# Reordering the last products of a convolution layer, and trimming idle products between layers, in a two-layer fp32 kernel

## The chip, the cores and the metric

The kernel runs on one core of a Trainium2 chip. The metric is the device time of one execution in microseconds (us). Three executions of the kernel before were timed; their median stands for it. A separate execution was profiled, and all instruction times below are from that one, counted from the start of its span.

## The reference, cut to what matters

```python
def reference(x, ...):                 # x: 32 images, 1024 channels, 14 x 14
    x = x + layer0(group_norm(x))      # three look-up products with softmax
    x = x + layer1(group_norm(x))      # linear attention and a depthwise 3x3
    return x

def layer0(x):
    out = relu(bn(amm(x, c1, lut1)))               # 1024 -> 256 channels
    out = relu(bn(amm(patches3x3(out), c2, lut2))) # 256 -> 256 channels
    return relu(bn(amm(out, c3, lut3)) + x)        # 256 -> 1024 channels

def amm(patches, centroids, lut):
    # per codebook: scores against 16 centroids, softmax, product with a table
    scores = 2 * einsum("blcs,cks->blck", v, centroids) - sum(centroids ** 2)
    return einsum("blck,cko->blo", softmax(scores), lut)
```

Batch normalisation takes its statistics over all images, so each of the three products of layer 0 must be complete before the next one can start. All is fp32.

The text calls the three products of layer 0 "layer 1", "layer 2" and "layer 3" of the kernel, as the code does, and the attention layer "layer 4".

## The kernel before, in words

**Units.** Layers 1 and 2 run over 16 pairs of images (392 positions) and, in each pair, over 8 blocks of 512 score rows: 128 units each, numbered u. For a unit, TensorE computes four score tiles of 128 x 392 (L874 in layer 1; L994 and L1003 in layer 2), called S(u) below. ScalarE takes their exponentials (L566). VectorE turns them so that the 16 scores of a codebook lie side by side (L578), sums them (L596), takes the reciprocal (L598) and turns that back (L604). GpSimd multiplies (L608); in layer 1 it also adds the two halves of the scores (L581) ahead of VectorE's sum. In units whose number divides by four GpSimd first writes a block of rows to a spare tile (L606). SyncE copies rows of the spare tile into every 16th row of the unit's tiles by DMA (L694), four copies or three. Then TensorE multiplies the unit with the table (L712), called L(u) below: eight matmuls, or six in every fourth unit, accumulated over the eight units of a pair. A matmul of fp32 shows as two instructions.

**Order.** Each engine executes its instructions in the order in which the program writes them, and `units` writes this order by hand: a loop over i in which S(i+4), the first transpose of unit i+3, the softmax of unit i+2 and L(i) follow each other in layer 1 (S(i+3), transpose and softmax of i+2, and L(i) in layer 2). `side(i)` hangs further work on the loop: group normalisation, and from i = 121 loads of layer 2's tables, 512 KB each, into the buffers that layer 1's tables leave.

**Between layers 1 and 2.** After L(127) come batch statistics, scale and bias (L749, L310 to L327). `store_pair(p, h)` writes the normalised map of a pair into a padded tile on ScalarE (L904) and sends it to DRAM in three DMAs (L915). `load_patches` reads the shifted maps back (L935), on SyncE's queue and, for the first unit, on ScalarE's too. In the list `luts2[b]`, entry 1 loads a table, entry 2 subtracts its last rows from the others with two matmuls and two copies on ScalarE (L669, L670), entry 3 keeps a piece of it in DRAM (L673) and entry 4 loads pieces from there (L676). Score biases need one more matmul (L388) and several small operations on VectorE, which also makes the score matrices w8 (L349) and wm (L975).

**Between layers 2 and 3.** `relu3(k, b)` normalises one chunk of 448 positions on ScalarE (L1078), `score3` computes four score tiles (L1088) and their exponentials. The products of layer 3 are at L1123.

**Layer 4** begins with residual, normalisation statistics and group normalisation of the first pair. Its instructions are put in order by a planner (`Plan`), which gives each piece a rank and an assumed duration and lets each engine take the ready piece of the lowest rank.

**Products nobody reads.** `warm(n, rhs)` writes n matmuls of the identity with some tile (L561; L1344 in layer 4). Their results aren't used.

Of the kernel before, what the change touches and what calls it, by code (L numbers as in the profile page):

```python
# [21 lines left out]
N2 = 2 * HW  # L22
# [128 lines left out]
def conv_preact_kernel(ctx: ExitStack, tc: tile.TileContext, a: dict, out: bass.AP):  # L151
# [3 lines left out]
    NP = B // 2  # L155
# [335 lines left out]
    def layers(exact, early=None):  # L491
# [20 lines left out]
        pads = [  # L512
            big.tile([P, 2 * IMG], F32, tag=f"pad{k}", name=f"pad{k}") for k in range(2)
        ]
# [42 lines left out]
        def warm(n, rhs):  # L557

            t = scores(rhs.shape[1])
            for _ in range(n):  # L560
                nc.tensor.matmul(t, ident, rhs, start=True, stop=True)  # L561
# [131 lines left out]
            for j in range(0 if q else 1, 4):  # L693
                nc.sync.dma_start(t[15::16, j, :N2], kept[4 * q + j - 1 :: 16])  # L694

        def units(ahead, ts, pool, luts, score, bias, dst, stats, side, last, halve=False):

            n = 8 * NP  # L700
            po, late, tts = [], [], {}

            def lut(u):
                p, b = divmod(u, 8)
                if b == 0:
                    po[:] = [
                        ps_po.tile([P, 512], F32, tag="po", name="po")[:, :N2] for h in range(2)
                    ]
                j0 = 0 if b % 4 else 1
                order = [(h, j) for h in range(2) for j in range(j0, 4)]  # L710
                for h, j in order if b == 7 else sorted(order, key=lambda k: k[1]):
                    nc.tensor.matmul(  # L712
                        po[h],
                        luts[b][:, j, h * P : (h + 1) * P],
                        ts[u % len(ts)][:, j, :N2],
                        start=(b == 0 and j == j0),
                        stop=(b == 7 and j == 3),
                    )
                if b == 7:
                    for h in range(2):  # L720
                        o = dst[:, h, p * N2 : (p + 1) * N2]
                        nc.scalar.copy(o, po[h])
                        late.append((stats[:, h, p, :], o))

            for i in range(-ahead, n):
                u = i + ahead
                if u < n:
                    scs = score(u)
                    exponentials(ts[u % len(ts)], scs, bias[:, 4 * (u % 8) :][:, :4])
                u = i + ahead - 1  # L730
                if 0 <= u < n:
                    tts[u] = token_major(pool, ts[u % len(ts)], halve)
                u = u - 1 if halve else u
                if 0 <= u < n:
                    softmax(
                        pool,
                        u,
                        ts[u % len(ts)],
                        *tts.pop(u),
                        spare=spares[u // 4 % 2] if u % 4 == 0 else None,  # L740
                    )
                    spare_rows(ts, u)
                while late:
                    nc.vector.bn_stats(*late.pop(0))
                side(i)
                if i >= 0:
                    lut(i)
            for h in range(2):
                nc.vector.bn_stats(*late.pop(0))  # L749
                last(h)  # L750
# [4 lines left out]
        with ExitStack() as s:  # L755
# [55 lines left out]
            luts2 = [packed_lut(2, b) for b in range(8)]  # L811
# [19 lines left out]
            luts = [packed_lut(1, b) for b in range(8)]  # L831
# [24 lines left out]
            ts = unit_tiles(AHEAD + 2)  # L856
# [11 lines left out]
            def score1(u):  # L868
# [18 lines left out]
                side,  # L887
                lambda h: bn_final(once, stats1, 1, [h], sc1, bi1),
                halve=not exact,
            )  # L890
            add_up(0, 8 * NP)


        with ExitStack() as s:
# [48 lines left out]
            luts2[0][2]()  # L943
            luts2[0][3]()
            luts2[1][2]()
            luts2[7][1]()
            load_patches(0, 0, 1, engines=(nc.sync, nc.scalar))
            store_pair(0, 1)
            luts2[2][2]()
            load_patches(0, 1, 3)  # L950
            luts2[3][2]()
            for b in range(4):
# [14 lines left out]
            )  # L967
            w8 = score_matrices(once, 2, "8", raw8, mask64)
            biases()
            warm(5, pads[0][:, :N2])  # L970

            centre(once, 2, "1", raw1, 2.0)
            wm = once.tile([P, 2, 4, P], F32, tag="wm", name="wm")
# [38 lines left out]
            ahead = 1 if exact else 3  # L1012
# [28 lines left out]
            out2 = out1  # L1041
# [19 lines left out]
        with ExitStack() as s:  # L1061
            once = s.enter_context(tc.tile_pool(name="p3c", bufs=1))
            stats3 = once.tile([P, CT, NCH, 6], F32, tag="stats3", name="stats3")
            mv3 = once.tile([P, CT, 2], F32, tag="mv3", name="mv3")
            again = None
            sf = s.enter_context(tc.tile_pool(name="p3t", bufs=4))
            st = s.enter_context(tc.tile_pool(name="p3tt", bufs=2))
            ap = s.enter_context(tc.tile_pool(name="p3a", bufs=2))
            luts = luts3
            w3, bias3 = parts[3]  # L1070

            def chunk(k, b):
                return out2[:, b, k * NC : (k + 1) * NC]

            def relu3(k, b):
                if k < NCH:
                    v = chunk(k, b)
                    nc.scalar.activation(  # L1078
                        v, v, AF.Relu, bias=bi2[:, b : b + 1], scale=sc2[:, b : b + 1]
                    )  # L1080

            def score3(k, b):
                v = chunk(k, b)
                scs = []
                for j in range(4):
                    sc = scores(NC)
                    r = slice(32 * j, 32 * j + 32)
                    nc.tensor.matmul(  # L1088
                        sc, w3[r, b, :], v[r], start=True, stop=True
                    )  # L1090
                    scs.append(sc)
                t = sf.tile([P, 4, NC], F32, tag="t", name="t")
                exponentials(t, scs, bias3[:, 4 * b : 4 * b + 4])
                return t

            for k, b in ((0, 0), (0, 1), (1, 0), (1, 1)):
                relu3(k, b)
            warm(7, out2[:, 0, :N2])
            t3, nxt = [score3(0, 0), score3(0, 1)], [score3(1, 0)]
            warm(5, out2[:, 0, :N2])  # L1100
            for b, t in enumerate(t3):
                softmax(st, b, t, *token_major(st, t))
            for k in range(NCH):
                more = k + 1 < NCH
                if more and k:
                    nxt = [score3(k + 1, 0)]
                elif not more and not exact:
                    add_up(2, 2 * NCH)
                    again = overflow(once)
                if early and k > 0:  # L1110
                    early.pop(0)(ps_tr)
                o = ap.tile([P, CT, NC], F32, tag="o3", name="o3")

                for ms in ((0, 1, 2), *((m,) for m in range(3, CT))) if k == 0 else (
                    (m,) for m in range(CT)
                ):
                    pos = [
                        ps_po.tile([P, 512], F32, tag="po", name="po3")[:, :NC] for m in ms
                    ]
                    for h in range(2):  # L1120
                        for m, po in zip(ms, pos):
                            for g in range(4 * h, 4 * h + 4):
                                nc.tensor.matmul(  # L1123
                                    po,
                                    luts[g][:, m * P : (m + 1) * P],
                                    t3[h][:, g % 4, :],
                                    start=(g == 0),
                                    stop=(g == 7),
                                )
                    for m, po in zip(ms, pos):  # L1130
                        nc.scalar.copy(o[:, m, :], po)  # L1131
                        nc.vector.bn_stats(stats3[:, m, k, :], o[:, m, :])  # L1132
                        if not more:
                            bn_sum(mv3[:, m, :], stats3, m)
                        if more and m == 0:
                            nxt.append(score3(k + 1, 1))
                        if m in (4, 5):
                            relu3(k + 2, m - 4)
                        if more and m in (1, 3):
                            t = nxt[m // 2]  # L1140
                            softmax(st, 2 * k + 2 + m // 2, t, *token_major(st, t))
                nc.sync.dma_start(o3d[:, :, k * NC : (k + 1) * NC], o)
                t3 = nxt
            bn_final(once, None, 3, range(CT), sc3, bi3, mv3)
# [20 lines left out]
    with ExitStack() as s:  # L1165
# [188 lines left out]
        def group_norm(p, h, rank):  # L1354
# [3 lines left out]
            key = lambda n: (n, p % 2, h)  # L1358
# [44 lines left out]
            do(DVE, rank, 0.1, variance, [pv], [key("gve")])  # L1403
            if p == 0 and h == 1:

                for n, need in ((16, []), (10, [key("gve")])):
                    warm(n, need)
            do(
                POOL, rank, 1.9, scale, [key("gve"), key("nmc")], [key("ga"), key("gb")], port=True
# [338 lines left out]
        def store(p, h, xt, rank):  # L1748
# [23 lines left out]
            key=8.5,  # L1772
# [176 lines left out]
```

## Time and profile before

| what | value |
|---|---|
| median of 3 runs | 3738.24 us (3735.01 to 3738.82) |
| the profiled execution | 3735.15 us, its span 3733.4 us |
| granted TensorE clock, mean | 0.994 |
| TensorE busy (matmuls) | 3640.7 us, 98% |
| VectorE busy | 2981.7 us, 80% |
| GpSimd busy | 2303.4 us, 62% |
| ScalarE busy | 1715.1 us, 46% |
| layer 1's last product ends | 835.6 us |
| layer 2's first and last products | 875.28 us, 1840.7 us |
| layer 3's first product, and its end | 1861.51 us, 2569.7 us |

A line of the timeline reads: start in us, length in us, engine, line of the kernel, operation, output <- input, shape, number of instructions, and in brackets the idle time ahead of it with what ended it. SPq and ACTq are the DMA issues on SyncE's and ScalarE's queues. A granted clock of 1.00 is TensorE's full speed. Where several instructions stand in one line, its length is that of the whole group.

### The profile page before, as it was taken

To read this page: it belongs to the slowest core of one execution; us is meant where nothing else is said; L and a number is where in the kernel's file an instruction comes from. 1 tells how busy PE (TensorE), PEld (TensorE's weight loads), DVE (VectorE), ACT (ScalarE), POOL (GpSimd) and SP (SyncE) were. 2 spreads that over 40 slices of the span, in tenths; PEclk is the share of its full clock that TensorE was granted. 3 is DMA by queue.
4 is the path that set the end of the run, shared out by engine and by line. 5 is a ranking of instruction groups with operands and counts; after the bars stand their busy time and mean duration, and the time that the engine had idled before them with its cause. 6 is when DMAs were issued, how large, how long until landed. Compare 5 with 4: busy or idle time off the path is not lost. (4 is left out here: it accounts for less than half of the span.)

```text
span 3733.4 us, 49281 instructions
## 1 busy us (share of the span) xinstructions
PE 3640.7 (98%) x16231; PEld 2030.0 (54%) x16231; DVE 2981.7 (80%) x4287; ACT 1715.1 (46%) x3883; POOL 2303.4 (62%) x1394
## 2 busy tenths in 40 slices
PE   8999999998999999999999999998999999999998
PEld 4555555554444444445444444445666666666665
DVE  8999999988888888888734333333699999999996
ACT  5555555543333333333312122213766676666774
POOL 6999999983445445445311111111988888878886
PEclk9999999999999999999999999999999999999999
DMA  3111111115343434344211111103133233322321
GB/s 109 43 46 44 43 43 37 32 54 128 82 94 79 94 78 94 79 97 83 62 40 48 40 40 40 40 22 131 33 87 94 77 86 89 86 85 82 89 74 44
DMA packets 235329, 256.51 MB, mean 69 GB/s; under 512 B 32240, under 2 KB 232816, under 8 KB 235064
## 3 DMA queue, kind: packets, MB, share of 16 engines
q1 hardware_dynamic: 234280, 252.88, 25.7%
q8 instruction: 132, 2.16, 0.3%
q14 instruction: 133, 1.09, 0.1%
q10 hardware_dynamic: 784, 0.37, 0.0%
HBM read 164.04 MB, written 77.09 MB: 65 GB/s over the span
## 5 line engine op out<-in xcount | busy, mean ns | idle before, releaser
L608 POOL TENSOR_TENSOR t<-t,r 128x1664 f32<-128x1664 f32 (+2 forms) x284 | 1006.8, 3545 | 975.5 <-DVE r L604 780.5
L712 PE MATMUL po<-t,lut 128*128 128x392 f32 x3840 | 1331.2, 499 | 5.1 <-DMA t<-spare 5.1
L712 PEld LDWEIGHTS po<-t,lut 128*128 128x128 f32 x3840 | 709.8, 190 | 594.9 <-issue 122.5
L566 ACT ACTIVATE t<-sc,cbias 128x392 f32<-128x392 f32 (+1 forms) x1136 | 579.1, 593 | 886.9 <-issue 480.5
L1459 PE MATMUL mm<-y,lut 128*128 128x392 f32 x2048 | 713.9, 495 | 2.8 <-ACT y L1425 1.7
L1123 PE MATMUL po<-t,lut 128*128 128x448 f32 x1792 | 680.6, 540 | 3.7 <-POOL t L608 2.1
L578 DVE STREAM_TRANSPOSE tt<-t 128x1664 f32<-128x1664 f32 (+1 forms) x284 | 541.9, 1908 | 111.8 <-ACT t L566 102.5
L604 DVE STREAM_TRANSPOSE r<-rc 128x1664 f32<-128x1664 f32 (+1 forms) x284 | 546.6, 1925 | 20.9 <-DVE rc L598 0.5
L1681 DVE SCALAR_TENSOR_TENSOR pa<-y,lepe_w,pa 128x406 f32<-128x406 f32 x900 | 538.9, 638 | 5.3 <-PE pa L1663 2.6
L1123 PEld LDWEIGHTS po<-t,lut 128*128 128x128 f32 x1792 | 338.2, 190 | 343.1 <-issue 340.3
L1459 PEld LDWEIGHTS mm<-y,lut 128*128 128x128 f32 x2048 | 370.4, 188 | 250.3 <-issue 8.0
L596 DVE TENSOR_REDUCE sm<-tt 128x104 f32<-128x832 f32 (+2 forms) x284 | 423.4, 1491 | 7.5 <-POOL tt L581 2.0
L1132 DVE BATCH_NORM_STATS2 stats<-o 128x6 f32<-128x448 f32 x112 | 69.0, 617 | 450.0 <-ACT o L1131 450.0
L581 POOL TENSOR_TENSOR tt<-tt 128x832 f32<-128x832 f32 x128 | 247.7, 1935 | 9.3 <-DVE tt L578 9.3
L1131 ACT COPY o<-po 128x448 f32<-128x448 f32 x112 | 59.0, 528 | 405.1 <-PE po L1123 359.1
L598 DVE RECIPROCAL rc<-sm 128x104 f32<-128x104 f32 (+1 forms) x284 | 229.5, 808 | 9.8
L994 PE MATMUL sc<-patch,cw 64*128 64x392 f32 x1024 | 204.9, 514 | 2.3 <-ACT lut L670 1.4
L609 ACT ACTIVATE sm<-sm 128x104 f32<-128x104 f32 (+1 forms) x284 | 84.8, 299 | 221.2 <-DVE rc L598 219.2
L1644 POOL TENSOR_TENSOR qr<-qr,zb 128x784 f32<-128x784 f32 x64 | 117.4, 1850 | 59.6 <-DMA zb<-zd 52.2
L1312 ACT ACTIVATE w<-x,tb,gn_a 128x196 f32<-128x196 f32 x248 | 128.3, 517 | 49.2 <-DVE x L1326 34.7
L994 PEld LDWEIGHTS sc<-patch,cw 64*128 64x128 f32 x1024 | 87.9, 184 | 110.8 <-issue 63.4
L606 POOL TENSOR_TENSOR spare<-t,r 128x392 f32<-128x392 f32 x64 | 65.1, 1017 | 120.1 <-DMA patch<-h1d 31.6
(189 smaller groups left out, 4090.3 us busy)
## 6 DMA issues: line engine op xcount, KB each, us to landing
patch<-h1d SPq DMA_DIRECT2D x248, 162.8 KB
x<-in_x_dram SPq DMA_DIRECT2D x32, 784.0 KB
o3d<-o SPq DMA_DIRECT2D x14, 1792.0 KB
x<-in_x_dram SPq DMA_DIRECT2D x64, 392.0 KB
out_dram<-x SPq DMA_DIRECT2D x64, 392.0 KB
o<-o3d SPq DMA_DIRECT2D x62, 392.0 KB
h1d<-pad SPq DMA_DIRECT2D x96, 225.0 KB
t<-spare SPq DMA_DIRECT2D x960, 12.2 KB
```

Of the source, the lines that this page charges most:

```text
L566: nc.scalar.activation(t[:, j, : sc.shape[1]], sc, AF.Identity if exact else AF.Exp, bias=bias[:, j : j + 1],)
L578: nc.vector.transpose(tt, tf)
L581: nc.gpsimd.tensor_tensor(tv[:, :, :8], tv[:, :, :8], tv[:, :, 8:], ALU.add)
L596: nc.vector.tensor_reduce(sm, tv, AX.X, ALU.add)
L598: nc.vector.reciprocal(rc, sm)
L604: nc.vector.transpose(r, bc(rc, 2, KC))
L608: nc.gpsimd.tensor_tensor(tf, tf, r, ALU.mult)
L712: nc.tensor.matmul(po[h], luts[b][:, j, h * P : (h + 1) * P], ts[u % len(ts)][:, j, :N2], start=(b == 0 and j == j0), stop=(b == 7 and j = ...
L994: nc.tensor.matmul(sc, w8[r, 8 * h + 4 * (j // 2) + g], grid(pbuf[n % NPB][r, j // 2, g]), start=True, stop=False,)
L1123: nc.tensor.matmul(po, luts[g][:, m * P : (m + 1) * P], t3[h][:, g % 4, :], start=(g == 0), stop=(g == 7),)
L1459: nc.tensor.matmul(pv(), w[kt][:, m0 : m0 + P], ywin(p, first + kt), start=(kt == 0), stop=(kt == 3),)
L1681: nc.vector.scalar_tensor_tensor(acc, neighbours(p, c, offset(k)), lw[:, c, k : k + 1], acc, ALU.mult, ALU.add,)
```

## The change

- `units` has a new argument `near`. In layer 1 (of the normal path) it is 8 x 16 - 12 = 116. Up to i = 115 the loop writes L(i) as before; at i = 116 it writes L(116) and L(117); after that it writes L(i+1). The statistics of the last outputs are held back in the last turn, so that they are written after the loop as before. In layer 2 `near` isn't given and the order stays.
- Between layers 1 and 2, `luts2[2][2]()` (two matmuls and two copies on ScalarE) moves ahead of the load of the eighth table, of the first patch loads and of `store_pair(0, 1)`. `warm(5)` ahead of the first scores goes.
- Between layers 2 and 3, `warm(7)`, which read the normalised map, becomes `warm(3)` on a table, ahead of everything; `relu3` of the second chunk goes behind the first chunk's scores and exponentials.
- In layer 4 the two groups of unread products have 12 and 9 instead of 16 and 10.

```diff
@@ units
-                while late:
+                while late and i < n - 1:
                     nc.vector.bn_stats(*late.pop(0))
                 side(i)
-                if i >= 0:
-                    lut(i)
+                near = n if near is None else near
+                for u in (i, i + 1) if i == near else (i + 1,) if i > near else (i,):
+                    if 0 <= u < n:
+                        lut(u)
@@ layer 1's call of units
                 halve=not exact,
+                near=None if exact else 8 * NP - 12,
@@ layer 1 to 2
             luts2[1][2]()
+            luts2[2][2]()
             luts2[7][1]()
             load_patches(0, 0, 1, engines=(nc.sync, nc.scalar))
             store_pair(0, 1)
-            luts2[2][2]()
             load_patches(0, 1, 3)
...
             biases()
-            warm(5, pads[0][:, :N2])
@@ layer 2 to 3
-            for k, b in ((0, 0), (0, 1), (1, 0), (1, 1)):
-                relu3(k, b)
-            warm(7, out2[:, 0, :N2])
-            t3, nxt = [score3(0, 0), score3(0, 1)], [score3(1, 0)]
+            warm(3, luts[0][:, :N2])
+            relu3(0, 0)
+            relu3(0, 1)
+            t3, nxt = [score3(0, 0), score3(0, 1)], []
+            relu3(1, 0)
+            relu3(1, 1)
+            nxt.append(score3(1, 0))
             warm(5, out2[:, 0, :N2])
@@ layer 4, group_norm
-                for n, need in ((16, []), (10, [key("gve")])):
+                for n, need in ((12, []), (9, [key("gve")])):
                     warm(n, need)
```

More of the change, by code (lines that the diff above doesn't have):

```diff
@@ L694, in spare_rows, with units @@
                 nc.sync.dma_start(t[15::16, j, :N2], kept[4 * q + j - 1 :: 16])
-        def units(ahead, ts, pool, luts, score, bias, dst, stats, side, last, halve=False):
+        def units(
+            ahead, ts, pool, luts, score, bias, dst, stats, side, last, halve=False, near=None
+        ):
             n = 8 * NP
```

## The prediction

> Below, S(u) is the four score matmuls of unit u and L(u) its products with the table; times are us from the span's start.
>
> **What bounds the kernel now.** The page's first part has PE busy for 98% of the span, so a gain must come from where PE stops or is fed late. I read the timeline engine by engine at the four places edited. PE, end of layer 1 and start of layer 2:
>
> ```profile
> 773.65 5.50 PE L712 MATMUL po<-t,lut 128*128 128x392 f32 x16 [0.22 <-DMA t<-spare]
> ...
> 809.45 0.94 PE L874 MATMUL sc<-x,cw 32*128 32x392 f32 x8
> 810.32 25.28 PE L712 MATMUL po<-t,lut 128*128 128x392 f32 x76
> 835.44 6.17 PE L669 MATMUL less<-lut,less_last 128*128 128x512 f32 x14
> 846.89 2.08 PE L669 MATMUL less<-lut,less_last 128*128 128x512 f32 x2 [5.28 <-ACT lut L670]
> 848.76 1.90 PE L388 MATMUL pb<-croom 72*128 72x512 f32 x2
> 850.47 3.49 PE L561 MATMUL sc<-pad,ident 128*128 128x392 f32 x10
> 853.89 1.59 PE L994 MATMUL sc<-patch,cw 64*128 64x392 f32 x8
> ```
>
> The first line is L(117), waiting for its row copies; S(127) and the last five L follow. From 773.65 to 835.6 PE never stops: reordering this stretch can't shorten it. Then PE stops for 5.28 behind ACT, and 3.49 go to a product nobody reads. What feeds L is POOL's multiplication, then SP's row copies (POOL here for units 117 and 127, then SP for 127):
>
> ```profile
> 768.06 3.73 POOL L608 TENSOR_TENSOR t<-t,r 128x1664 f32<-128x1664 f32 x1
> ...
> 822.37 3.70 POOL L608 TENSOR_TENSOR t<-t,r 128x1664 f32<-128x1664 f32 x1 [0.31 <-DVE r L604]
> ```
> ```profile
> 826.09 2.59 SPq L694 DMA_DIRECT2D t<-spare  x4
> ```
>
> Between the layers, ACT stands behind its own DMA issues, with copies queued behind it:
>
> ```profile
> 841.32 4.29 ACTq L935 DMA_DIRECT2D patch<-h1d  x6
> 845.65 0.71 ACT L904 ACTIVATE pad<-out,bi,sc 128x392 f32<-128x392 f32 x1 [6.00 <-DMA patch<-h1d]
> 846.27 1.54 ACT L670 COPY lut<-less 128x512 f32<-128x512 f32 x3
> ```
>
> Layer 2 to 3 (ACT, then PE), and layer 3 to 4 (PE, then DVE):
>
> ```profile
> 1843.86 2.06 ACT L1078 ACTIVATE out<-out,bi,sc 128x448 f32<-128x448 f32 x3 [1.88 <-DVE bi L327]
> 1847.95 4.41 ACT L566 ACTIVATE t<-sc,cbias 128x448 f32<-128x448 f32 x8 [2.02 <-issue]
> ```
> ```profile
> 1861.51 18.31 PE L1123 MATMUL po<-t,lut 128*128 128x448 f32 x48 [2.15 <-POOL t L608]
> ```
> ```profile
> 2579.45 9.63 PE L1344 MATMUL mm<-tb,ident 128*128 128x256 f32 x32 [9.75 <-DVE tb L1180]
> 2588.92 0.51 PE L1368 MATMUL mm<-gst,gavg 128*128 128x8 f32 x4
> ```
> ```profile
> 2587.08 0.62 DVE L1331 BATCH_NORM_STATS2 gst<-x 128x6 f32<-128x196 f32 x2
> ```
>
> [...]in stretches of 1 us (length, busy PE, PE loads, DVE, ACT, POOL, then granted clock, DMA share, GB/s):
>
> ```profile
> 844.00:845.00 1.00, 0.00 (x0) 0.00 (x0) 1.00 (x2) 0.00 (x0) 0.00 (x0) 0.50 0.33 97
> 850.00:851.00 1.00, 1.00 (x3) 0.39 (x2) 0.30 (x1) 0.00 (x0) 0.00 (x0) 0.74 0.84 210
> ```
>
> PE is empty from 841.6, and the clock is at 0.50 from about 843.9 to 850.7. [...]POOL's end at 771.79 to L(117)'s start took 1.86, which I use.
>
> **Part 1, L moved ahead: a loss of 7.4.** From i=116 each L(i+1) runs ahead of S(i+5). L(117) is wanted at 772.5, but its rows land at 773.65, so S(121) goes from 772.49 to 779.12. Each later S then has one more L before it. A unit's chain from S: 3.06 to DVE's first transpose (809.45 to 812.51); that transpose, then the preceding unit's reduction, reciprocal and second transpose take 5.6 in DVE's order; POOL 3.7; rows 1.86. So L(u-1) can start 14.2 after S(u) starts. PE has before it S(u), L(u-3), S(u+1), L(u-2), S(u+2): three S at 0.87 and two L at 5.47 (4.15 where a unit has three row blocks), 12.2 to 13.5. Unit by unit (POOL's end plus 1.86, against PE free): L(120) 791.6, so 793.45 against 792.67, waits 0.8; L(121) 797.8, 799.65 against 798.47, 1.2; L(122) 804.3, 806.15 against 805.99, 0.2; L(123) none; L(124) 817.6, 819.5 against 818.83, 0.7. S(127) starts at 818.0 rather than 809.45, and after it no S is left to fill. L(125) waits 2.2 for POOL until 825.85. L(126) may start at 818.0+14.2=832.2, 0.9 late. L(126) and L(127), unbroken, take 5.32 each: end 842.8, against 835.4. Cover assumed: 512 KB weight loads issued between row copies are gone before the next. The statistics of the last outputs, held back for the end, are the same two instructions at the same place after L(127): nothing. Ends: +4 if the waits at units 120 to 124 vanish, +9 if weight loads delay rows.
>
> **Part 2, layer 1 to 2: a gain of 3.5.** Relative to L(127)'s end, written in before's times. Two less-copies leave ACT's queue behind the DMAs and run at 840 to 841.4, while ACT would wait anyway for the map's write (landed 841.3); ACT's six issues slip 0.1. The moved call issues two products on PE and no DMA; SP's queue keeps its order. PE's last less-product ends at 842.5 rather than 848.97, the bias product at 844.4, DVE's bias and wm at 848.9 rather than 854.38. S(0) then waits for its patches, issued until 845.6, landed near 848: 6 earlier. But S(1)'s patches (SP, 12 issues from 848.25) aren't earlier: DMA share falls from about 0.85 to 0.60 only at 857. S(1)'s fourth matmul goes at 858.3 instead of 859.4, its exponentials at 859.2 instead of 860.67. Gone too is ACT's wait of 1.98 for DVE's second reciprocal (DVE starts 4 earlier), so S(3) ends near 869.3 instead of 872.8 and L(0) starts near 871.7 instead of 875.28. Patches of map 1, which held PE 0.85 at 881.76, follow SP 4 earlier. The removed 5 products cost 3.49, part of this sum. They covered the clock: now PE stands nearly idle from 844.4 to 848 and S(0) may run at half clock, 2.5 more, which the wait for S(1)'s patches hides; cover gone, the gain falls. Ends: -5 and 0.
>
> **Part 3, layer 2 to 3: a gain of 3.3.** Three products of a resident table start with L(127)'s end, 1840.7 to 1842.7, waiting for nothing new; S(0,0) follows at once. ACT does two maps, not four, then the exponentials: second map 1843.86 to 1844.6, exponentials from 1844.6 instead of 1847.95, so DVE, POOL and the first L1123 come 3.35 earlier. The other two maps go behind eight exponentials (to 1848.9); S(1,0) waits, and nobody needs it before 1861. POOL's second half is ready at 1865, PE wants it at 1867. The 5 remaining unread products still end before 1858.2. Ends: -3.6 and -1 (first L1123 at half clock).
>
> **Part 4, layer 3 to 4: a gain of 0.7.** A warm 256-wide product is 4.56/10=0.456. Statistics are ready at 2587.70, PE at 2588.92: four fewer (1.8) end before them, and L1368 starts at 2587.75, 1.17 earlier. DVE is then busy until 2588.71, so the chain moves 0.76. One fewer in the second group only keeps it ahead of the second statistics. The planner's queue has nothing ready on PE in those slots, so its order should stay. Ends: -1.2 and 0.
>
> **Sum**: +7.4-3.5-3.3-0.7=-0.1: span 3733.3, run 3735.0 by the profiled execution's 3735.15. The median of the runs is 3.1 above that execution: 3738.1.
>
> **Rivals.** (a) *Half clock through layer 2's fill* (slower). For it: row-sliced scores left clock at 0.50 from 1850.8 to 1857.7 while PE had work. Against: scores and less-products held 1.00 from 850.7 to 883. S(0) to the last less-product is 17.7 of work; all at half clock from 848, L(0) starts at 883, 8 late: part 2 is +8, total +11.4, 3750. It decides (7.5) from 13.6 of that work cold. (b) *The row copies keep up*: part 1 costs 3, total -4.5, 3734; at nothing, -7.5, 3731. For: in before most L start without waiting; against: L(117) already waits 0.22. (c) *The gains are absorbed*: patches land later, layer 4's loads (DMA share 1 until 2602) hold; parts 2 and 4 give 1, total +3, 3741. That the code does less than it says is excluded: each edit changes program order of engines written in order.
>
> **How the numbers follow.** Main case 0.50, all within 0.2% (7.5 us, about what a measurement can tell from no change). (a) 0.14, slower. (b) 0.20, of which 0.14 faster. (c) 0.16, of which 0.06 slower. Faster 0.14, same 0.66, slower 0.20. Range 3730 to 3746: it holds (b), (c) and the ends that can coincide, and leaves out (a).
>
> **What would show it.** PE waits of 1 to 2 before the last L of layer 1, S(127) some 8.5 later; in layer 2 no 5.28 wait, PE empty before S(0) with the clock near 0.5, L(0) 36 after the last L of layer 1 instead of 39.7; first L1123 17.5 after layer 2's end instead of 20.8. L without waits would make part 1 wrong; a cold clock through the fill, part 2.

## The result, and the profile after

The changed kernel took 3755.11 us (median of 6 runs, 3750.86 to 3758.32). The kernel before, timed beside it, took 3738.53 us (6 runs, 3735.01 to 3741.91). The ratio is 1.0042, 95% interval [1.0031, 1.0053]: slower by 0.42%, outside the range of 3730 to 3746. The profiled execution has a span of 3749.3 us, 15.9 more than before.

All line numbers of the changed kernel are a few higher than in the kernel before: L(u) is L714 instead of L712, layer 1's scores L878, layer 2's L998 and L1007, ScalarE's map L909, layer 3's products L1130, unread products of layer 4 L1351, its copies L1531.

The timeline of TensorE (PE) in the kernel after, end of layer 1 and start of layer 2:

```profile
773.97 5.50 PE L714 MATMUL po<-t,lut 128*128 128x392 f32 x16 [1.08 <-DMA t<-spare]
...
793.83 4.19 PE L714 MATMUL po<-t,lut 128*128 128x392 f32 x12 [0.81 <-DMA t<-spare]
...
800.13 5.50 PE L714 MATMUL po<-t,lut 128*128 128x392 f32 x16 [1.24 <-DMA t<-spare]
...
818.32 0.94 PE L878 MATMUL sc<-x,cw 32*128 32x392 f32 x8
820.05 4.19 PE L714 MATMUL po<-t,lut 128*128 128x392 f32 x12 [0.79 <-POOL tt L581]
826.39 5.50 PE L714 MATMUL po<-t,lut 128*128 128x392 f32 x16 [2.15 <-POOL tt L581]
832.70 10.77 PE L714 MATMUL po<-t,lut 128*128 128x392 f32 x32 [0.80 <-DMA t<-spare]
843.30 7.03 PE L669 MATMUL less<-lut,less_last 128*128 128x512 f32 x16
850.17 1.02 PE L388 MATMUL pb<-croom 72*128 72x512 f32 x2
853.88 3.23 PE L998 MATMUL sc<-patch,cw 64*128 64x392 f32 x8 [2.69 <-DMA patch<-h1d]
...
868.74 1.69 PE L1007 MATMUL sc<-pad,wm 32*128 32x392 f32 x8
870.36 3.75 PE L669 MATMUL less<-lut,less_last 128*128 128x512 f32 x4
...
884.09 4.11 PE L714 MATMUL po<-t,lut 128*128 128x392 f32 x12
```

The first six L714 lines with a bracket are the waits of part 1: L(117), L(120), L(121), L(124), L(125), L(126). The 5.28 behind ScalarE is gone; in its place PE waits 2.69 for the first unit's patches. The line at 870.36 takes 3.75 for what took 1.98 before: the clock is low there, at 0.50 from 868 to 873. In stretches of 1 us (PE, PE loads, DVE, ACT, POOL, then granted clock, DMA share, GB/s):

```profile
851.00:852.00 1.00, 0.19 (x1) 0.00 (x0) 1.00 (x3) 0.00 (x0) 0.00 (x0) 1.00 0.86 238
854.00:855.00 1.00, 1.00 (x4) 0.47 (x4) 0.93 (x5) 1.00 (x3) 0.00 (x0) 0.50 0.45 121
868.00:869.00 1.00, 1.00 (x6) 0.26 (x8) 0.00 (x0) 0.00 (x0) 1.00 (x2) 0.50 0.77 99
```

The timeline of ScalarE there, whose copies now stand ahead of its DMA issues (844.64, issues from 849.53) and in the kernel before stood behind them (846.27, issues from 841.32):

```profile
844.64 1.16 ACT L670 COPY lut<-less 128x512 f32<-128x512 f32 x2
...
849.53 4.29 ACTq L940 DMA_DIRECT2D patch<-h1d  x6
853.87 0.72 ACT L909 ACTIVATE pad<-out,bi,sc 128x392 f32<-128x392 f32 x1 [4.63 <-DMA patch<-h1d]
```

Layer 2 to 3 (ScalarE, then PE) and layer 3 to 4 (PE):

```profile
1848.02 0.76 ACT L1082 ACTIVATE out<-out,bi,sc 128x448 f32<-128x448 f32 x1 [1.87 <-DVE bi L327]
1848.68 4.77 ACT L566 ACTIVATE t<-sc,cbias 128x448 f32<-128x448 f32 x8
```
```profile
1862.22 18.31 PE L1130 MATMUL po<-t,lut 128*128 128x448 f32 x48
```
```profile
2581.89 8.16 PE L1351 MATMUL mm<-tb,ident 128*128 128x256 f32 x24 [9.75 <-DVE tb L1187]
2590.20 0.61 PE L1375 MATMUL mm<-gst,gavg 128*128 128x8 f32 x4 [0.15 <-DVE gst L1338]
```

All four parts can be seen. Marks at the borders of the layers, in the two profiles:

| mark, us from the span's start | before | after | shift |
|---|---|---|---|
| layer 1's last product ends (start of the one after it) | 835.44 | 843.30 | +7.9 |
| layer 2's last product ends | 1840.69 | 1844.84 | +4.2 |
| layer 3's first product | 1861.51 | 1862.22 | +0.7 |
| layer 4's first product | 2596.94 | 2598.52 | +1.6 |
| end of the span | 3733.40 | 3749.30 | +15.9 |

At layer 4's first product the changed kernel is 1.6 us late. It loses 14.3 us after that, where the edited text has nothing more to do. The table of waits, PE from 2605 us on, of the kernel before:

```profile
PE mm L1521 <- ACT kt L1524: 11.2, 7, 2.4
PE pa L1663 <- DVE x L1695: 2.5, 2, 2.0
```

and of the kernel after (us in total, times, the longest):

```profile
PE mm L1528 <- ACT kt L1531: 24.5, 17, 2.5
PE mm L1466 <- DVE q L1483: 3.6, 2, 2.0
PE mm L1528 <- DVE q L1483: 2.0, 1, 2.0
```

PE waits 17 times instead of 7 for the same ScalarE copies, and newly for VectorE's `q`; all its waits there come to 33.6 instead of 21.4. That is more than one late step that shifts the rest: the order of layer 4 is another. GpSimd's timeline shows it at the end. Before, the four multiplications by `zb` run together, after everything else; after, there are rotations of `q` between the third and the fourth. The kernel before:

```profile
3696.24 1.00 POOL L1718 TENSOR_TENSOR x<-x,side 128x392 f32<-128x392 f32 x1
3704.72 7.26 POOL L1644 TENSOR_TENSOR qr<-qr,zb 128x784 f32<-128x784 f32 x4 [7.48 <-ACT zb L1650]
```

The kernel after:

```profile
3708.10 5.51 POOL L1651 TENSOR_TENSOR qr<-qr,zb 128x784 f32<-128x784 f32 x3
3713.54 1.75 POOL L1511 TENSOR_TENSOR ru<-q,sinq 128x784 f32<-128x784 f32 x1
...
3718.28 1.84 POOL L1651 TENSOR_TENSOR qr<-qr,zb 128x784 f32<-128x784 f32 x1
```

So the question was not where the gains of the change went, but what gave layer 4 another order. The planner lets each engine take its next piece in a loop over

```python
engines = {p[0] for p in self.pieces}
...
for e in engines:
```

The names are strings in a Python set, and such a set's order isn't fixed: it can differ from one build of the same text to the next. Where two engines want pieces that exclude each other (those marked `port`), the one asked first gets its own. That is the code's rule; the runs below test the order as a whole, not this rule by itself.

### The profile page after: what moved, and what is told of

It is laid out like the page before. It is cut to its first block, busy times and chain, and to the rows that moved or that the text cites. A ratio compares the mean times of both kernels' runs of the same rounds, so it can differ in the third digit from the quotient of the medians.

```text
span 3749.3 us, 49207 instructions
## 1 busy us (share of the span) xinstructions
PE 3642.6 (97%) x16203; PEld 2031.2 (54%) x16203; DVE 2994.7 (80%) x4287; ACT 1713.3 (46%) x3883; POOL 2304.5 (61%) x1394
## 3 DMA queue, kind: packets, MB, share of 16 engines
q14 instruction: 133, 1.09, 0.1%
## 5 line engine op out<-in xcount | busy, mean ns | idle before, releaser
L714 PE MATMUL po<-t,lut 128*128 128x392 f32 x3840 | 1331.9, 499 | 10.7 <-DMA t<-spare 7.6
L714 PEld LDWEIGHTS po<-t,lut 128*128 128x128 f32 x3840 | 709.7, 190 | 601.2 <-issue 129.2
L1130 PE MATMUL po<-t,lut 128*128 128x448 f32 x1792 | 682.3, 542 | 1.7 <-issue 1.6
L604 DVE STREAM_TRANSPOSE r<-rc 128x1664 f32<-128x1664 f32 (+1 forms) x284 | 546.6, 1925 | 20.8 <-DVE rc L598 0.5
L1688 DVE SCALAR_TENSOR_TENSOR pa<-y,lepe_w,pa 128x406 f32<-128x406 f32 x900 | 541.8, 639 | 20.3 <-PE pa L1670 17.6
L1130 PEld LDWEIGHTS po<-t,lut 128*128 128x128 f32 x1792 | 338.9, 190 | 342.1 <-issue 341.3
L998 PE MATMUL sc<-patch,cw 64*128 64x392 f32 x1024 | 207.7, 518 | 5.7 <-DMA patch<-h1d 5.7
L1651 POOL TENSOR_TENSOR qr<-qr,zb 128x784 f32<-128x784 f32 x64 | 117.7, 1851 | 68.4 <-DMA zb<-zd 68.2
L998 PEld LDWEIGHTS sc<-patch,cw 64*128 64x128 f32 x1024 | 88.8, 185 | 116.2 <-issue 66.4
L1475 ACT ACTIVATE e<-mm,kbd 128x392 f32<-128x392 f32 x128 | 74.1, 579 | 164.7 <-PE mm L1466 163.5
```

The costliest lines, as they stand in the source:

```text
L604: nc.vector.transpose(r, bc(rc, 2, KC))
L714: nc.tensor.matmul(po[h], luts[b][:, j, h * P : (h + 1) * P], ts[u % len(ts)][:, j, :N2], start=(b == 0 and j == j0), stop=(b == 7 and j = ...
L998: nc.tensor.matmul(sc, w8[r, 8 * h + 4 * (j // 2) + g], grid(pbuf[n % NPB][r, j // 2, g]), start=True, stop=False,)
L1130: nc.tensor.matmul(po, luts[g][:, m * P : (m + 1) * P], t3[h][:, g % 4, :], start=(g == 0), stop=(g == 7),)
L1688: nc.vector.scalar_tensor_tensor(acc, neighbours(p, c, offset(k)), lw[:, c, k : k + 1], acc, ALU.mult, ALU.add,)
```

## Experiments

In all kernels below the set is replaced by a list, so their order is fixed ("pinned"). None leaves out a part of the computation.

### 1. Is it the order of the set?

Two theories. The first: the set's order alone makes layer 4 slow, whatever the change does. The second: the change starts layer 4 at another moment, and its loads collide. Four kernels: before and after, each with GpSimd asked first (`b_pool`, `a_pool`) and with VectorE asked first (`b_dve`, `a_dve`).

```diff
-        engines = {p[0] for p in self.pieces}
+        engines = ["POOL", "DVE", "PE", "ACT", "SP"]      # b_pool, a_pool
+        engines = ["DVE", "POOL", "PE", "ACT", "SP"]      # b_dve, a_dve
```

> The kernel before, with one line of the planner changed: it asks the engines for work in a fixed order, GpSimd ahead of VectorE, instead of in the order of a set of names, which two builds of one text can have differently. Nothing is left out. Theory 1 (the extra time of the changed kernel's layer 4 comes from another order of its pieces, chosen by that set): this is the order that the profiled kernel before had, so a span of 3733 and about 3737 in the runs. Theory 2 (the shifted start of layer 4 brings its loads into another's way): the same 3737, since nothing of the change is in.

> The kernel before, the planner's order fixed with VectorE ahead of GpSimd, which is the order that the changed kernel's profile shows. Theory 1: layer 4 takes some 14 us longer than in b_pool, so 3748 to 3752, slower than before without any edit of the change. Theory 2: within 2 us of b_pool, 3737.

> The whole change, planner's order fixed with GpSimd ahead of VectorE. Theory 1: the change by itself costs what the profile shows up to layer 4's first product, 1.6 us, so 3737 to 3741 and the same as b_pool within 3 us. Theory 2: 3751 to 3755 as in the run of the change.

> The whole change, planner's order fixed with VectorE ahead of GpSimd. Theory 1: b_dve plus 1.6 us, 3750 to 3755, as in the run of the change. Theory 2: 3751 to 3755 too; the two differ in b_dve and a_pool.

| kernel | median us (lowest to highest, runs) | span of the profiled run | layer 4's first product to the end |
|---|---|---|---|
| before, GpSimd first | 3738.90 (3737.56 to 3740.97, 6) | 3735.8 | 1136.2 |
| after, GpSimd first | 3743.49 (3737.45 to 3744.78, 11) | 3736.9 | 1138.0 |
| before, VectorE first | 3756.54 (3752.21 to 3761.85, 12) | 3750.6 | 1152.7 |
| after, VectorE first | 3757.30 (3749.70 to 3764.65, 12) | 3762.9 | 1158.3 |

The unchanged kernel with VectorE first is as slow as the changed one was, and the changed kernel with GpSimd first is back within 5 us of the one before. Three of the four times lie above the ranges expected (3743.5 against 3737 to 3741, 3756.5 against 3748 to 3752, 3757.3 against 3750 to 3755), but each is on the side of the first theory. The waits of `b_dve` and of `a_pool` (each the first line of that table) are those of the other kernel:

```profile
PE mm L1521 <- ACT kt L1524: 24.6, 17, 2.6
```
```profile
PE mm L1528 <- ACT kt L1531: 11.8, 7, 2.5
```

The traces show which order the two kernels of the result had. From 15 us before layer 4's first unread product to the end, the 2518 instructions of VectorE, the 1655 of ScalarE and the 867 of GpSimd follow one another in the kernel before exactly as in `b_pool` and `a_pool`, and in the kernel after exactly as in `b_dve` and `a_dve`. Of the orders that five names can have, only these two were tried.

There was a control that nobody had planned. The kernel before, its text untouched, was built anew as the base of this series and of the two below. It now took 3756.19 us (32 runs), 3753.94 (23) and 3755.53 (10), where it had taken 3738.53. There is no profile of these builds; that they have the slower order is inferred from their times. So ratios to that base mix an edit with the draw of the order; the comparisons below are between pinned kernels. The first theory holds; the second falls: started between 2596.9 and 2599.6 with GpSimd first, and between 2597.9 and 2604.6 with VectorE first, layer 4 is short in the one order and long in the other, and in the unchanged kernel too.

Why it costs that much can be read a little further. The clock, in two stretches of the kernel after:

```profile
3280.00:3285.00 5.00, 4.66 (x20) 4.24 (x21) 5.00 (x10) 3.99 (x8) 2.04 (x3) 0.66 0.35 99
3686.00:3694.00 8.00, 6.39 (x15) 3.54 (x14) 5.42 (x11) 3.36 (x9) 6.29 (x6) 0.57 0.00 1
```

PE has work there, at a mean of 0.66 and 0.57 of its clock. In stretches of 1 us each such fall lasts 3.4 us at half clock (3.40 to 3.42) or twice that (6.82 to 6.84); counted as if PE were busy throughout, that is an estimate of 1.7 or 3.4 us of work lost. Summed over layer 4 in stretches of 1 us, GpSimd first has none to three such falls (0 to 5.1 us), VectorE first two to six (5.1 us in `after`, 8.5 in `b_dve`, 11.9 in `a_dve`). With this estimate taken off, layer 4 takes 1136.2 to 1139.2 us with GpSimd first in all profiles of this study, and 1144.1 to 1146.4 with VectorE first. So, pair by pair, 8 to 9 us go with the order's longer waits, and the rest with the clock. Why the clock falls more often in the slower order was not tested; that its longer waits bring this about is likely, not shown.

### 2. What the four parts are worth alone

With the order pinned to GpSimd first, each part by itself, beside the base timed again. `p1_alone` has the edit of `units`; `p2_alone` moves `luts2[2][2]()` and drops `warm(5)`; `p34_alone` has the edits at layer 3 and layer 4.

```diff
p1:   ...
      +                for u in (i, i + 1) if i == near else (i + 1,) if i > near else (i,):
      ...
p2:   +            luts2[2][2]()          # ahead of luts2[7][1]()
      -            warm(5, pads[0][:, :N2])
p34:  +            warm(3, luts[0][:, :N2])
      +            relu3(0, 0)
      +            relu3(0, 1)
      +            t3, nxt = [score3(0, 0), score3(0, 1)], []
      ...
      -                for n, need in ((16, []), (10, [key("gve")])):
      +                for n, need in ((12, []), (9, [key("gve")])):
```

> The kernel before with its planner asking GpSimd first, timed again beside the single parts below. If the order of the planner's set is all that moved layer 4, its time is that of the earlier run of the same program, 3736 to 3742 us, and layer 4 (first product to the end of the span) takes 1136 to 1138 us. If the earlier 3738.9 was chance and layer 4 varies from run to run, it lies anywhere from 3736 to 3757 us.

> The kernel before, GpSimd first, with the reordering of layer 1's last products alone. Theory (the parts' sum holds, layer 4 is not touched by them): the last product of layer 1 ends 7.3 to 7.8 us later than without the edit, all else shifts by the same, the time is 7.5 us above the kernel before in this order, about 3746. Rival (a later start of layer 4 makes it longer, or layer 2's fill takes the shift back): 3 us or less above it, or over 11.

> The kernel before, GpSimd first, with the edit between layers 1 and 2 alone (two subtractions of table rows earlier, five unread products gone). Theory: the first product of layer 2 starts 40.8 us after layer 1's last one, against 43.3 in this order before: a gain of 2.5 us, less than the 3.5 forecast because the patches of the second unit land no earlier and scores run at half clock. Rival (the 39.8 of the first profile is what the program before usually takes, and the edit is worth nothing or costs 1): 40.8 against 39.8, time equal to the kernel before or 1 us above it.

> The kernel before, GpSimd first, with the edits between layers 2 and 3 and between 3 and 4 alone. Theory: first product of layer 3 starts 17.4 us after layer 2's end instead of 20.8, first product of layer 4 starts 16.6 us after the first unread one instead of 17.6: 4.4 us less, about 3734.5. Rival (layer 4's loads hold its start, and what layer 3 gains comes back there): no change at the end of the span, about 3738.9.

| kernel | median us (lowest to highest, runs) | part's own mark | mark without the edit |
|---|---|---|---|
| `b_pool_2` | 3738.81 (3737.31 to 3739.47, 4) | | |
| `p1_alone` | 3746.72 (3743.00 to 3753.26, 20) | layer 1's last product ends 105.4 after the last L279 product (737.5), at 842.91 | 97.9, at 835.20 |
| `p2_alone` | 3738.59 (3735.72 to 3742.31, 4) | second product of layer 2 starts 47.5 after layer 1's last | 50.4 |
| `p34_alone` | 3737.57 (3734.65 to 3738.79, 4) | layer 3: 17.4 after layer 2; layer 4: 16.6 after its first unread product | 20.8; 17.6 |

Layer 4 takes 1138.7 us in `b_pool_2`'s profile, with one fall of the clock, where 1136 to 1138 were expected. Part 1 costs 7.5 us by its mark and 7.9 in the median: as expected. (The mark is taken from PE's last product of the group normalisation, L279, ahead of the reordering; without the edit it is 97.9 us in all nine profiles.) Parts 2, 3 and 4 show at their marks: `p2_alone`'s first product of layer 2 starts 41.1 us after layer 1's last one, where 40.8 was expected and `b_pool_2` has 43.3, and the marks of `p34_alone` are those expected. The times don't bear them out: the medians fall by 0.2 and 1.2 only, not by 2.5 and 4.4, which is nearer to the rivals of both expectations. The profiles of `p2_alone` and `p34_alone` each have two falls of the clock in layer 4 (3.4 us by the estimate above), that of `b_pool_2` one (1.7). And `p34_alone`'s profile is 3.9 us behind `b_pool_2`'s at that L279 product already, ahead of every edit. Falls in layer 4 show in five of the seven profiles of changed kernels with GpSimd first and in one of the four of the unchanged kernel; whether that is chance or follows from the change, so few profiles can't tell. With four runs of each, which lie 2 to 7 us apart, the medians can't settle gains of this size. The marks show the gains where they arise, not that they last to the end of the span.

For part 2 the first product of layer 2 is a poor mark: it starts 39.8 us after layer 1's last one in the first profile of the kernel before, 43.3 in `b_pool` and `b_pool_2`, for the same instructions, since the clock falls at different moments there. The second product is somewhat steadier (48.0, 50.5, 50.4). That first profile was a fortunate draw: five of the seven profiles with an unedited fill have a second fall of the clock some 37 us after layer 1's last product, as the subtraction of table rows that starts 39 to 40 us after it shows (3.77 or 3.78 instead of 1.98), and it has none. The timeline of PE in `b_pool`, where the first profile has 1.98 (at 873.46):

```profile
875.70 3.78 PE L669 MATMUL sc<-lut,less_last 128*128 128x512 f32 x4 [0.64 <-ACT t L566]
```

### 3. Without the edit of layer 1, and with less of it

`p234` is the change without part 1; `p234_warm_kept` also keeps the five unread products; `whole_near_122` is the whole change with the reordering begun six units later.

```diff
p234_warm_kept:  as p234, but
                 +            warm(5, pads[0][:, :N2])
whole_near_122:  -                near=None if exact else 8 * NP - 12,
                 +                near=None if exact else 8 * NP - 6,
```

> The kernel before, GpSimd first, as the base for the three kernels below. Two earlier series had medians of 3738.9 and 3738.8 us; the same is expected, 3737 to 3741, with the clock falling for some 20 us at one or two places of layer 4, other ones in each execution, 1 to 2 us each.

> The whole change without its edit of layer 1, GpSimd first. Theory (the parts add up and layer 4 gives nothing back): first product of layer 4 at 2592 to 2593 us from the span's start against 2599 in this order before, time 6 to 7 us less than the kernel before in this order, about 3732. Rival (layer 4 gives the gain back, as the single parts, whose medians fell by 0.2 and 1.2 only, would have it): first product at 2593, but time within 2 us of 3738.8.

> As the kernel without the edit of layer 1, but the five unread products ahead of layer 2's first scores stay. If the gain between the layers comes from the earlier subtractions and the unread products only fill a wait that is there anyway and keep the clock up, the first product of layer 2 starts no later than without them, within 40.1 to 41.5 us after layer 1's last one, and scores of the first units run faster (0.94 us for eight matmuls of 32 rows, not 1.69). If the unread products stand in the way, it starts 1.5 us or more later, at 42.5 or more.

> The whole change, GpSimd first, but the products of layer 1 follow by a unit less from unit 122 on, not from 116. By the working of part 1 (a unit's products can start 14.2 us after its scores; waits at L(117) and at units 120 to 122 come from putting more scores behind products): L(117) to L(122) no longer wait, the scores of unit 127 start near 815, the products of units 122 to 127 run on without a wait, and layer 1's last product ends within 1.5 us of the kernel before, near 836 to 837. Rival (moving the last scores behind one product costs what it did, wherever it begins): 840 or later. Time as for the kernel without the edit of layer 1, plus 0 to 1.5 us, or plus 5 and more.

| kernel | median us (lowest to highest, runs) | layer 1's last product ends | layer 4's first product | span |
|---|---|---|---|---|
| `b_pool_3` | 3737.05 (3736.55 to 3741.94, 5) | 834.81 | 2598.90 | 3735.2 |
| `p234` | 3735.70 (3734.47 to 3739.05, 5) | 835.54 | 2593.31 | 3733.9 |
| `p234_warm_kept` | 3733.72 (3729.20 to 3736.39, 5) | 836.31 | 2590.06 | 3727.4 |
| `whole_near_122` | 3742.23 (3741.81 to 3747.71, 6) | 841.73 | 2597.61 | 3740.0 |

The base's time is as expected; of the one or two falls of the clock expected in its layer 4, its profile shows none. (Where they show, they last 3.4 or 6.8 us, not the 20 of the expectation.)

**Fewer unread products can cost the clock.** `p234` gained 5.6 us up to layer 4's first product where 6 to 7 were expected. Its time missed: 3735.70 where about 3732 was expected, 1.4 us below `b_pool_3` and not 6 to 7. That most of the gain is gone at the end is what the rival had said; in the profile, two falls of the clock in layer 4 (3.4 us) go with it. What is missing ahead of layer 4's first product is in part 4. The timeline of PE of `p234`:

```profile
2573.99 6.82 PE L1346 MATMUL mm<-tb,ident 128*128 128x256 f32 x24 [9.73 <-DVE tb L1182]
2582.30 0.61 PE L1370 MATMUL mm<-gst,gavg 128*128 128x8 f32 x4 [1.48 <-DVE gst L1333]
2583.89 1.02 PE L1370 MATMUL mm<-gq,gavg 128*128 128x8 f32 x4 [0.98 <-DVE gq L1380]
2584.76 6.96 PE L1346 MATMUL mm<-tb,ident 128*128 128x256 f32 x18
```

and of `p234_warm_kept`, whose instructions here are the same:

```profile
2573.44 7.96 PE L1347 MATMUL mm<-tb,ident 128*128 128x256 f32 x24 [9.78 <-DVE tb L1183]
2581.74 0.61 PE L1371 MATMUL mm<-gst,gavg 128*128 128x8 f32 x4 [0.35 <-DVE gst L1334]
2583.33 0.61 PE L1371 MATMUL mm<-gq,gavg 128*128 128x8 f32 x4 [0.98 <-DVE gq L1381]
2583.80 4.13 PE L1347 MATMUL mm<-tb,ident 128*128 128x256 f32 x18
```

In `p234` the clock came up earlier (2.9 us after the start of these products, against 5.1), so the first twelve products were done 1.1 us sooner, and PE stood idle 1.48 and 0.98 us, with little between. Then the clock fell, and the next nine took 6.96 instead of 4.13. A stretch of 1 us of each (`p234`, then `p234_warm_kept`):

```profile
2584.00:2585.00 1.00, 1.00 (x5) 1.00 (x6) 0.96 (x4) 0.00 (x0) 0.00 (x0) 0.50 1.02 418
```
```profile
2584.00:2585.00 1.00, 1.00 (x6) 0.87 (x6) 1.00 (x4) 0.00 (x0) 0.49 (x1) 1.00 1.03 414
```

From the first unread product to layer 4's first product it is 17.5 to 17.7 us in all seven profiles with 16 and 10 products. With 12 and 9 it is 16.6 in five profiles, and 19.3 and 19.4 in `p234` and `a_dve`. The edit gains 1.0 or loses 1.8.

**The five unread products between the layers.** With them, layer 2's first product starts 39.8 after layer 1's last one, without them 39.1; the second 46.2 and 45.5. The expectation's first half holds nearly, 0.7 later instead of no later; the 1.5 or more of the second half did not come. They keep the clock up for the first unit only: its matmuls with the patches take 1.71 and those with `pad` 0.94, against 3.47 and 1.69 in `p234`, but the second unit's with `pad` take 1.69 in both. So they are filler there, and neither help nor harm by more than these profiles differ. Between the two profiled spans lie 6.5 us, of which 2.7 come at layer 4's unread products and some 3.4 from the two falls in layer 4 that `p234` has. Between the medians lie 2.0; what of that is due to the five products isn't shown.

**Beginning the reordering later.** The expectation of `whole_near_122` failed: layer 1's last product ended at 841.73, the rival's 840 or later, not near 836. The waits that the reordering had brought at L(117) and at units 120 to 122 went, as worked out. The time, 6.5 us above `p234`, is the rival's too. A wait of 4.00 came, the timeline of PE:

```profile
815.19 0.94 PE L878 MATMUL sc<-x,cw 32*128 32x392 f32 x8
816.06 9.48 PE L714 MATMUL po<-t,lut 128*128 128x392 f32 x28
829.54 12.34 PE L714 MATMUL po<-t,lut 128*128 128x392 f32 x32 [4.00 <-DMA t<-spare]
```

and VectorE's:

```profile
818.25 1.91 DVE L578 STREAM_TRANSPOSE tt<-t 128x1664 f32<-128x1664 f32 x1 [6.00 <-ACT t L566]
820.09 0.98 DVE L596 TENSOR_REDUCE sm<-tt 128x104 f32<-128x832 f32 x1
```

VectorE turns unit 127 before it sums unit 126. So with S(127) late, L(126) is late too: S(127) at 815.19 plus 14.2 is 829.39, and L(126) started at 829.54. That is the very rule of the prediction's part 1, "L(u-1) can start 14.2 after S(u) starts"; the expectation of this run had put it on L(127) instead. Putting S(127) behind one more L costs 5.8 us in this profile (103.7 after the last L279 product against 97.9). The wait is 4.0 of them. Nearly all of the rest is the clock, which fell during the wait: the 32 matmuls at 829.54 take 12.34 where the kernel after has 10.77 for the same ones. A stretch of 1 us there:

```profile
830.00:831.00 1.00, 1.00 (x3) 0.36 (x3) 0.00 (x0) 0.00 (x0) 1.00 (x1) 0.50 0.07 22
```

So the later start takes away some 3 us of waits and gives 1.6 back to the clock. In `p1_alone` the clock did not fall there (its last three L take 5.50 and 10.77, as in the kernel after, where the clock is at 1.00), and the waits of 1.09, 0.82, 1.23, 0.78, 2.15 and 0.81 make up most of its 7.5.

**The best version.** `p234_warm_kept`: 3733.72 against 3737.05 for the pinned kernel before, and all its runs lie below all runs of that. Its profiled execution is the fastest of its five (3729.20), so its marks may flatter it. By ratios to the common base, 0.9941 [0.9928, 0.9955] against 0.9953 [0.9940, 0.9967], the two intervals overlap. So the 3.3 us stand on five runs of each, and are less than half of what the marks promise (first product of layer 4 at 2590.06 instead of 2598.90). It is 21 us below the changed kernel as that was timed first; 14 to 18 of these are the pinned order.

## Why the prediction was wrong

**The step that failed** is in part 4: "The planner's queue has nothing ready on PE in those slots, so its order should stay." Its reason was right: with the set's order pinned, the numbers of unread products change nothing else in the order. But it took for granted that the order is a property of the text. It can be drawn anew at each build, and the kernel after was built with the slower draw. That layer 4 stays as it is was a term put at nothing, for a reason that spoke of the unread products alone. The sum was made against layer 4 of one draw (1136.5 us) and judged on the other (1150.8). None of the rivals has it; the one on layer 4, (c), spoke of loads. The set was to be seen in the planner's code. Of the 16.6 us between the medians, the draw is 14 to 18 (`b_dve` over `b_pool` 17.6, `a_dve` over `a_pool` 13.8).

**The change itself**: with the order held, +4.6 us by the medians of `a_pool` and `b_pool`, +0.8 by those of `a_dve` and `b_dve`, both without an interval of their own. Both lie within the 7.5 us that the forecast called no change. The forecast for the main case, part by part:

| part | forecast | measured, at its mark |
|---|---|---|
| 1, L moved ahead | +7.4 | +7.5 (`p1_alone`, after), +8.2 (`a_pool`, `a_dve`, where the last three L take 0.7 more), from the last L279 product |
| 2, layer 1 to 2 | -3.5 | -2.8 (second product of layer 2; mean of 6 profiles with, 46.9, against 7 without, 49.6); -1.1 against the profile before (48.0) |
| 3, layer 2 to 3 | -3.3 | -3.4 (20.8 to 17.4, in every profile) |
| 4, layer 3 to 4 | -0.7 | -1.0 in five profiles, +1.8 in two |
| to layer 4's first product | -0.1 | +1.6 (after against before); -0.8 (`a_pool` against `b_pool`); +6.6 (`a_dve` against `b_dve`) |

**Part 1** was right wait by wait: worked out 0.8, 1.2, 0.7, 2.2, 0.9 for L(120), L(121), L(124), L(125), L(126); measured 0.81, 1.24, 0.79, 2.15, 0.80. S(127) was put at 818.0 and came at 818.32, in a profile that runs 0.3 later at that L279 product already (737.87 against 737.54). Rival (b), rows that keep up, is out. What the working of part 1 left out shows in two profiles, `a_pool` and `a_dve`: the last three L cost 0.7 more. That the clock fell there is inferred from the length of these products. In `a_pool` three L in a row, 5.50, 0.80 of waiting and 10.77 in the kernel after, take

```profile
825.63 17.73 PE L714 MATMUL po<-t,lut 128*128 128x392 f32 x48 [2.16 <-POOL tt L581]
```

**Part 2** was too large by 0.7 as a difference of means, and that it was so near was in part luck. The forecast worked out the new course from one profile and compared it with that same profile; against that one the gain is 1.1. The other 1.6 come from the base, which is slower in most profiles than in the one that was read. The wait behind ScalarE went, the first unit's scores came early (10.6 us after layer 1's last product, not 18.5), and the second unit's patches came no earlier (SyncE issues them from 13.2 us after it, 12.8 in the kernel before): so far as written. The term that was mis-sized is the one for the clock: half clock was to hit S(0) only, "which the wait for S(1)'s patches hides". It came back at 867.1 (0.50 from 868 to 873) for the second unit's last scores and a subtraction (3.75 instead of 1.98), past that cover. Rival (a), half clock through the whole fill at +8, came in part: between the first score and L(0) the clock is at half for 13.7 us in the kernel after (853.5 to 860.3 and 867.1 to 873.9). By its mean from 840 to 860 and from 860 to 880 it is at half for some 13.6 us in `p234` (0.74, 0.92) and in `whole_near_122` (0.83, 0.83). But so it is in the unchanged `b_pool_3` (0.83, 0.83). The line against it, "held 1.00 from 850.7 to 883", was the fortunate draw. "L(0) 36 after the last L of layer 1 instead of 39.7" missed: 40.8 in the kernel after, where the unchanged kernel has anything from 39.8 to 43.3.

**Part 3** was right. **Part 4** was right in five profiles of seven; its ends, -1.2 and 0, left out that the clock can fall once there are fewer products: the nine took 6.96 in `p234` and 4.13 in `p234_warm_kept`. A loss was not in them. One reading bears on parts 2 and 4: in the kernel before, PE is empty from 841.6 and the clock at half from 843.7 (0.85 on average from 843 to 844, 0.50 from 844 on), 2.1 us later. So an idle stretch of 2.1 us wasn't safe there; how short one must be to be safe isn't shown.

## What to carry to other kernels

Where a kernel's order comes out of a program, look for what isn't fixed in it (sets, hash order, ties) before forecasting: a kernel and its change must be compared with that order held, and the same text built twice is the control. A sum of small parts read from a timeline can come out to within a microsecond or two at its marks while the end of the span is decided elsewhere, so lay two profiles side by side at marks between stages before explaining a total. Unread products that fill a wait can also hold TensorE's clock: with 12 and 9 of them it fell in two of seven profiles, and the edit lost 1.8 us there instead of gaining 1.0. Before taking some away, work out the idle time that this opens on both sides of the next short product.

## What was not expected of the hardware

The falls of TensorE's clock come in few lengths: each one in layer 4 lasted 3.4 us at half clock (3.40 to 3.42) or 6.8 (6.82 to 6.84), by estimate 1.7 us of work or twice that, and layer 4 with GpSimd first is 1136 to 1139 us plus 0 to 3 times 1.7. They come at different places from one execution to the next (2752, 3071, 3133 us), and most often start between 3413 and 3427, in six of eleven profiles with GpSimd first. The clock also fell after idle stretches of no more than 1.48 and 0.98 us with a group of four short matmuls (0.61 us) between them, in two of seven profiles with the same instructions there. And it fell where PE was hardly idle: in the kernel before at 1850.6 (0.81 on average from 1850 to 1851, then 0.50), after 7.6 us, from 1843.0 on, in which PE stopped for 0.65 us only; from 1846.85 on these were score matmuls of 32 rows. What share of work keeps the clock up isn't settled here.
